# The queue that issues six stores in the opening of a gather, state-space and convolution kernel

## The chip, the core and the metric

The kernel runs on one NeuronCore of a Trainium2 chip. The core has five engines with an instruction queue each: TensorE (PE) multiplies matrices into PSUM, VectorE (DVE) and ScalarE (ACT) compute on PSUM and SBUF, GpSimd (POOL) computes on SBUF, and SyncE (SP) issues transfers. Each queue is worked off in order. Transfers between HBM and SBUF (DMAs) run on 16 DMA engines; in this kernel SP, ScalarE and GpSimd issue them.

The metric is the time of one execution in device microseconds. It was 1114.07 us in the median of three executions (1113.97 to 1115.91).

## The reference

The input `x` holds 64 batches of 128 channels by 2048 steps, all in float32. Two residual layers follow each other:

```
W = weights[condition]                         # one of 16 matrices [128, 128] for each batch
x = x + einsum('bct,bcd->bdt', x, W)           # layer 0
K = 2 Re( sum_n Ct[h,n] exp(dtA[h,n] * l) )    # layer 1: a kernel of 2048 taps for each channel
y = causal convolution of x with K, + x * D
x = x + y * (step < length[batch])
```

Layer 0 multiplies each batch by a matrix that an index selects. Layer 1 is a state-space layer: its convolution kernel is a sum of 64 damped exponentials for each channel.

## The kernel before

The 2048 steps are cut into two segments of 1024. Layer 0 is done batch by batch, and its result is written to a scratch tensor in HBM (`scr`) in a layout that the second layer reads by channel. Layer 1 works on eight-channel groups that it loads back from `scr`, with the states carried from chunk to chunk. TensorE does its transposes, its products with the Toeplitz matrix of near taps and its reads of the states.

The change touches the opening stage, in which segment 0 of layer 0 runs for all 64 batches and the tables of layer 1 are made beside it. The function `batch0(b)` is one batch of it:

- For an even `b` it calls `fetch` (line 443): SP issues the load of a pair of batches, 1 MB, that is used 18 batches later. Load number n holds batches 2n and 2n+1. There are ten such buffers (`big`, ten of tag `x`), so load n reuses the buffer of load n-10 and must wait until the stores of both its batches have landed.
- `weigh` (line 457): GpSimd copies the selected matrix of a later batch.
- `project` (lines 468 and 473 to 478): TensorE multiplies into a PSUM tile of two banks (tag `y`, two buffers), the function `copy` brings the result back into the batch's place in SBUF (line 475), and a DMA stores it to `scr` (line 478, 0.5 MB).

The copy is ScalarE's, except for batches 12 to 17, where it is VectorE's. In these six turns of the loop ScalarE computes tables of exponentials, two tables of four instructions each turn (`exps`, line 499, 48 instructions in all), and VectorE computes partial angles (`partial_angles`, lines 648 to 661). From batch 18 on a pipeline of small steps (`STEPS`) makes the sine tables, two batches to a table: TensorE transposes (line 666), ScalarE copies to `a` (line 670), TensorE multiplies (line 677), VectorE reduces the angles (lines 685 to 688), ScalarE takes the sines (lines 692 and 693), and so on.

The order of the work on each engine is that of the program. Semaphores between engines are placed by the compiler. For the DMAs that SP and ScalarE issue it has eight completion semaphores, which it gives out in turn in the order of issue; an issue waits until the DMA that had its semaphore before has landed.

The loop around the change, which calls `batch0` for batches 12 to 63, chooses the copying engine by the batch's number:

```
for now in range(12, B):
    batch0(now, V.tensor_copy if now < 18 else nc.scalar.copy)
    ...
    if now < 18:
        exps(2 * now - 20)
        exps(2 * now - 19)
```

Of the kernel before, what the change touches and what calls it, by code (L numbers as in the profile page):

```python
# [46 lines left out]
F32 = mybir.dt.float32  # L47
# [6 lines left out]
P = 128  # L54
# [322 lines left out]
def cond_resid_ssm_kernel(  # L377
# [13 lines left out]
    nc = tc.nc  # L391
# [9 lines left out]
    BK = 512  # L401
# [18 lines left out]
    psp = ctx.enter_context(tc.tile_pool(name="psp", bufs=1, space=PSUM))  # L420
# [14 lines left out]
    QB = SL // BK  # L435
# [3 lines left out]
    def fetch(s, n):  # L439

        xbs[s, n] = big.tile([P, BT, SL], F32, tag="x", name=f"xb_{s}_{n}")
        src = x[n * BT : (n + 1) * BT, :, s * SL : (s + 1) * SL]
        nc.sync.dma_start(xbs[s, n], src.rearrange("b c t -> c b t"))

    def weigh(s, b, plus=None):

        w1s[s, b] = s0.tile([P, C], F32, tag="w1", name=f"w1_{s}_{b}")
        at = nc.values_load(
            ci[:, b : b + 1],
            engines=(mybir.EngineType.Pool,),  # L450
            min_val=0,
            max_val=S - 1,
            skip_runtime_bounds_check_because="it is clamped above",
        )
        w = wres[:, bass.ds(at, 1), :].rearrange("p s d -> p (s d)")
        if plus is None:
            nc.gpsimd.tensor_copy(w1s[s, b], w)  # L457
        else:
            nc.gpsimd.tensor_tensor(w1s[s, b], w, plus, ALU.add)

    def project(s, b, q, ps, n_banks=1, copy=nc.scalar.copy):

        n, r = divmod(b, BT)
        own = xbs[s, n][:, r, :]
        for k in range(n_banks):
            cols = [slice((q + j) * BK, (q + j + 1) * BK) for j in (k, n_banks - 1 - k)]
            if s > 0:
                nc.tensor.matmul(ps[:, k], w1s[s, b], own[:, cols[0]], start=True, stop=True)  # L468
                continue

            for h in range(2):
                c = slice(h * B, (h + 1) * B)
                nc.tensor.matmul(ps[c, k], w1s[s, b][:, c], own[:, cols[h]], start=True, stop=True)  # L473
        cols = slice(q * BK, (q + n_banks) * BK)
        copy(own[:, cols], ps.rearrange("p k t -> p (k t)"))  # L475
        if q + n_banks == QB:
            to = scr[s].rearrange("(f b) c t -> b c f t", f=2)[b]
            nc.scalar.dma_start(to, own.rearrange("c (f t) -> c f t", f=2))
            del w1s[s, b]
            if r == BT - 1:  # L480
                del xbs[s, n]

    def batch0(b, copy=nc.scalar.copy):
        if b % BT == 0 and b // BT + AHEAD < B // BT:
            fetch(0, b // BT + AHEAD)
        if b + WAHEAD < B:
            weigh(0, b + WAHEAD)
        project(0, b, 0, psp.tile([P, QB, BK], F32, tag="y", name=f"p0_0_{b}", bufs=2), QB, copy)

    V = nc.vector  # L490
    es = [tab.tile([P, TP, 2, NE], F32, tag=f"e{g}", name=f"e_{g}") for g in range(NT)]
# [4 lines left out]
    def exps(g):  # L496

        for i in range(TP):
            nc.scalar.activation(es[g][:, i, 0, :], steps, AF.Exp, scale=par_of(DRE, g, i))
# [12 lines left out]
    with tc.tile_pool(name="setup", bufs=1) as setup:  # L512
# [93 lines left out]
        for b in range(3):  # L606
            batch0(b)
        par.sines()
        run(others)
        batch0(3)  # L610
        par.lay("ppar_1", rows, 3, par.row(gtab, DRE))
        run(par.gains())
        phases = _weave(par.phases(), masks(), par.steps_of_chunk())
        for b in range(4, 10):
            batch0(b)
            run(phases, 12)
            if b >= 6:
                exps(b - 6)
# [20 lines left out]
    def partial_angles(k):  # L639

        own = parts[:, :, 0:NL]
        by_l = some_l.unsqueeze(1).to_broadcast([P, NP, NL])

        def of(row, n):
            return gtab[:, row, :].unsqueeze(2).to_broadcast([P, NP, n])

        if k == 0:
            V.tensor_tensor(own, of(FHI, NL), by_l, ALU.mult)
        elif k == 1:
            V.tensor_scalar(whole, own, MAGIC, MAGIC, ALU.add, ALU.subtract)  # L650
        elif k == 2:
            V.tensor_tensor(own, own, whole, ALU.subtract)
        elif k == 3:
            V.tensor_tensor(whole, of(FLO, NL), by_l, ALU.mult)
        elif k == 4:
            V.tensor_tensor(own, own, whole, ALU.add)
        else:
            V.tensor_tensor(parts[:, :, 0:8], parts[:, :, 0:8], of(PHI, 8), ALU.add)
            V.tensor_tensor(parts[:, :, 24:25], parts[:, :, 24:25], of(PHI, 1), ALU.add)
            V.tensor_scalar(last, parts[:, :, 24:25], MAGIC, MAGIC, ALU.add, ALU.subtract)  # L660
            V.tensor_tensor(last, parts[:, :, 24:25], last, ALU.subtract)
# [76 lines left out]
    def some(n):  # L738
        nonlocal done
        for s, b, q in pieces[done : done + n]:  # L740
            weights_for(done + WAHEAD * QB + 1)
            project(s, b, q, psp.tile([P, 1, BK], F32, tag="tr", name=f"p0_{s}_{b}_{q}", bufs=2))
            done += 1

    def fetches(n):

        nonlocal begun
        while begun < min(n + BT * QB, len(pieces)):
            fetch(pieces[begun][0], pieces[begun][1] // BT)
            begun += BT * QB  # L750
# [9 lines left out]
    ps = {}  # L760
# [11 lines left out]
        0: turn_parts,  # L772
    }
    for now in range(12, B):
        batch0(now, V.tensor_copy if now < 18 else nc.scalar.copy)
        if now < 20:

            by_row = d_in.rearrange("(d c h j) -> c d j h", j=8, c=2, d=2)
            with nc.allow_non_contiguous_dma(reason="128 gains, four times"):
                for i, r in ((i, r) for i in range(TP) for r in range(4) if (i * 4 + r) // 2 == now - 12):  # L780
                    nc.gpsimd.dma_start(dcol[i * NR + r : (i + 1) * NR : 4, :], by_row[r % 2, r // 2])
        if now == 21:
            V.tensor_scalar(dcol, dcol, 1.0, None, ALU.add)
        if now < FIRST:
            partial_angles(now - 12)
# [3 lines that stand above are left out]
        for lag, step in STEPS.items():  # L789
            g, odd = divmod(now - FIRST - lag, 2)  # L790
            if not odd and 0 <= g < NT:
                step(g)
        if now == 60:
            fetches(FILL)
# [248 lines left out]
```

## Time and profile before

| | |
|---|---|
| median of three executions | 1114.07 us (1113.97 to 1115.91) |
| profiled execution: its own time | 1113.85 us |
| profiled execution: span | 1111.8 us |
| mean granted TensorE clock | 0.993 |
| busy: TensorE | 1070.2 us, 96% of the span |
| busy: VectorE | 817.7 us, 74% |
| busy: ScalarE | 679.9 us, 61% |
| busy: GpSimd | 226.9 us, 20% |
| DMA, mean over the span | 282 GB/s, 313.31 MB |
| stores to `scr` (line 478) | 128 of 0.5 MB, 7.8 us from issue to landing in the median |
| loads of pairs (line 443) | 64 of 1 MB, 9.6 us in the median |
| chain that ended last, by engine | TensorE 89%, DMA 6%, ScalarE 2%, VectorE 2% |

How to read it: times are counted from the start of the span. "Busy" leaves out instructions that only issue, branch or wait. The chain is followed back from the last instruction to what released it, or to the instruction before it on its engine. In the lists of instructions, columns are the start, the duration, engine, line, operation, what it writes and reads, the count, and in brackets the idle time before it with what ended it. "ACTq" and "SPq" are the queues of ScalarE and SP, in which DMAs are issued; "DMA scr<-xb" is a store, "DMA xb<-in_x_dram" a load.

### The profile page before, as it was taken

What the parts mean: (1) busy time and instruction counts of PE and PEld (TensorE: products, weight loads), DVE (VectorE), ACT (ScalarE), POOL (GpSimd) and SP (SyncE); (2) the same over time, 40 slices, a digit from 0 to 9 for tenths busy, and PEclk for the clock granted to TensorE, in tenths of its full rate; (3) what the DMA queues carried; (4) which work ended last, traced back from release to release, by engine and by line L of the source; (5) the groups of instructions that cost most, each with busy time, mean ns of one, the idle gap of its engine ahead of it and who ended that gap; (6) DMA issues with size and microseconds to landing.
All of it is one profiled execution on the core that took longest, in us unless ns stands there. A gap on an engine that the chain in (4) does not pass through costs nothing.

```text
span 1111.8 us, 24599 instructions
## 1 busy us (share of the span) xinstructions
PE 1070.2 (96%) x8890; PEld 756.9 (68%) x8890; DVE 817.7 (74%) x2902; ACT 679.9 (61%) x1119; POOL 226.9 (20%) x389
## 2 busy tenths in 40 slices
PE   4779999999999999999999999999999999999996
PEld 1223333667767777776776778788888888888885
DVE  7665650568667667766766868888888888888886
ACT  3576665666666666566666666555665566566552
POOL 3152342121121112122122111212111211111120
PEclk9799999999999999999999999999999999999999
DMA  9999999999999999999999877678777787888754
GB/s 345 414 398 397 386 383 369 402 332 284 353 297 292 298 314 287 306 311 289 294 306 299 255 236 230 213 210 246 223 219 219 241 229 212 229 235 228 208 166 119
DMA packets 142731, 313.31 MB, mean 282 GB/s; under 512 B 12882, under 2 KB 13010, under 8 KB 142610
## 3 DMA queue, kind: packets, MB, share of 16 engines
q1 hardware_dynamic: 96528, 218.65, 62.5%
q10 hardware_dynamic: 35106, 67.64, 15.9%
q0 software_dynamic: 10976, 25.45, 8.4%
q8 instruction: 70, 1.15, 0.4%
q14 instruction: 51, 0.42, 0.1%
HBM read 164.76 MB, written 146.93 MB: 280 GB/s over the span
## 4 chain that ended last, share of the span: by engine, by line
PE 89%; DMA 6%; ACT 2%; DVE 2%; issue 0%; ACTq 0%; SPq 0%; DVEq 0%
PE y L924 20%; PE y L916 20%; PE v L871 18%; PE tr L849 10%; PE p L468 9%; PE p L473 7%; DMA scr<-xb 3%; PE pb L832 2%; DMA xb<-in_x_dram 2%; PE pt L677 1%; DVE s L886 1%; ACT xb L475 1%; PE pk L707 1%; DMA x<-scr 1%; DVE x L946 1%; ACT s L876 0%
## 5 line engine op out<-in xcount | busy, mean ns | idle before, releaser
L886 DVE SCALAR_TENSOR_TENSOR s<-s,ptab 128x128 f32<-128x128 f32 x1792 | 536.5, 345 | 194.7 <-ACT s L876 194.5
L876 ACT ACTIVATE s<-v,ptab 64x512 f32<-64x512 f32 (+1 forms) x512 | 336.0, 656 | 52.0 <-PE v L871 34.9
L916 PEld LDWEIGHTS y<-tt,u 128*128 128x128 f32 x2048 | 263.5, 192 | 80.5 <-issue 67.0
L916 PE MATMUL y<-tt,u 128*128 128x128 f32 x2048 | 269.9, 275 | 0.1
L924 PEld LDWEIGHTS y<-e,s 64*128 64x128 f32 (+1 forms) x4096 | 219.0, 181 | 52.1 <-issue 27.2
L871 PE MATMUL v<-u,bt 128*128 128x512 f32 (+1 forms) x512 | 248.7, 567 | 1.3 <-ACT u L850 1.0
L850 ACT COPY u<-tr 128x512 f32<-128x512 f32 x252 | 148.1, 588 | 152.1 <-PE tr L849 125.6
L924 PE MATMUL y<-e,s 64*128 64x128 f32 (+1 forms) x4096 | 237.3, 276 | 1.4 <-DVE s L886 1.4
L475 ACT COPY xb<-p 128x512 f32<-128x512 f32 (+1 forms) x186 | 133.5, 718 | 85.9 <-PE p L468 54.4
L946 DVE COPY_PREDICATED x<-mask,y 128x1024 f32<-128x1024 uint8 x128 | 166.7, 1303 | 1.0 <-PE y L924 1.0
L849 PE MATMUL tr<-ident,x 128*128 128x128 f32 x1024 | 155.5, 274 | 1.2 <-DVE u L850 0.8
L849 PEld LDWEIGHTS tr<-ident,x 128*128 128x128 f32 x1024 | 121.2, 141 | 50.9 <-issue 44.9
L473 PE MATMUL p<-xb,w 128*64 128x512 f32 x512 | 126.0, 629 | 19.4 <-DMA xb<-in_x_dram 11.1
L457 POOL COPY w<-wres 128x128 f32 x125 | 56.7, 454 | 429.4 <-PE p L468 315.4
L468 PE MATMUL p<-xb,w 128*128 128x512 f32 x256 | 129.6, 596 | 0.9 <-issue 0.6
L473 PEld LDWEIGHTS p<-xb,w 128*64 128x64 f32 x512 | 35.4, 143 | 88.6 <-issue 84.9
L871 PEld LDWEIGHTS v<-u,bt 128*128 128x128 f32 x512 | 79.5, 191 | 15.9 <-issue 13.4
L818 POOL DMA_DIRECT2D tt<-kpad x64 | 50.5, 789 | 194.3 <-DVE s L886 158.3
L896 DVE TENSOR_SCALAR s<-s 128x64 f32<-128x64 f32 x448 | 87.8, 196 | 0.0
L859 POOL DMA_DIRECT2D s<-carry x64 | 44.9, 706 | 127.0 <-PE y L924 114.4
L833 ACT COPY bt<-pb 128x512 f32<-128x512 f32 x32 | 18.8, 586 | 79.3 <-PE pb L832 75.6
L907 POOL DMA_DIRECT2D carry<-s x64 | 43.6, 724 | 100.1 <-DVE s L886 88.3
(205 smaller groups left out, 390.1 us busy)
## 6 DMA issues: line engine op xcount, KB each, us to landing
xb<-in_x_dram SPq DMA_DIRECT2D x64, 1024.0 KB, 9.6
scr<-xb ACTq DMA_DIRECT2D x128, 512.0 KB, 7.8
x<-scr SPq DMA_DIRECT2D x64, 1024.0 KB, 8.2
out_dram<-x SPq DMA_DIRECT2D x130, 256.0 KB, 3.6
out_dram<-x SPq DMA_DIRECT2D x62, 512.0 KB, 4.6
tt<-kpad POOLq DMA_DIRECT2D x64, 256.0 KB, 5.7
btd<-bt SPq DMA_DIRECT2D x32, 256.0 KB, 5.2
bt<-btd SPq DMA_DIRECT2D x32, 256.0 KB, 4.8
```

Of the source, the lines that this page charges most:

```text
L468: nc.tensor.matmul(ps[:, k], w1s[s, b], own[:, cols[0]], start=True, stop=True)
L473: nc.tensor.matmul(ps[c, k], w1s[s, b][:, c], own[:, cols[h]], start=True, stop=True)
L475: copy(own[:, cols], ps.rearrange("p k t -> p (k t)"))
L849: nc.tensor.transpose(tr[:, k, :], xs[i][:, n, k * Q : (k + 1) * Q], ident)
L850: (nc.vector.tensor_copy if i == 0 else nc.scalar.copy)(u, tr)
L871: nc.tensor.matmul(v[:, 0:nv], w, us[i, n].rearrange("p k r -> p (k r)")[:, 0:nv], start=True, stop=True)
L876: nc.scalar.activation(own[:, 0:nv], v[lanes, 0:nv], AF.Copy, scale=amp)
L886: nc.vector.scalar_tensor_tensor(new, src, factor, own, ALU.mult, ALU.add)
L896: nc.vector.tensor_scalar(old[d][:, 2], old[d][:, 0], -1.0, None, ALU.mult)
L916: nc.tensor.matmul(y[:, k, :], u[:, k, :], tts[i][:, n, :], start=(k == 0), stop=False, skip_group_check=True)
L924: nc.tensor.matmul(ys[i, d][rows, c, k, :], ss[i][half[c], d, part, k, :, :].rearrange("p f b -> p (f b)")[:, rows], es[pair // TP][half[c ...
L946: nc.vector.copy_predicated(xs[i][:, 2 * d : 2 * d + 2, :].rearrange("r c (k t) -> r c k t", k=KK), keep_k.unsqueeze(1).to_broadcast([P, 2 ...
```

## The change

The six stores of batches 12 to 17 are issued by SP. The function `project` gets a parameter for the queue that issues the store, `batch0` hands it on, and the loop passes `nc.sync` for the batches that VectorE copies. The copies, the loads, the sizes and the order of everything else in the program stay as they are.

```diff
-    def project(s, b, q, ps, n_banks=1, copy=nc.scalar.copy):
+    def project(s, b, q, ps, n_banks=1, copy=nc.scalar.copy, queue=nc.scalar):
 ...
         if q + n_banks == QB:
             to = scr[s].rearrange("(f b) c t -> b c f t", f=2)[b]
-            nc.scalar.dma_start(to, own.rearrange("c (f t) -> c f t", f=2))
+            queue.dma_start(to, own.rearrange("c (f t) -> c f t", f=2))
 ...
-    def batch0(b, copy=nc.scalar.copy):
+    def batch0(b, copy=nc.scalar.copy, queue=nc.scalar):
 ...
-        project(0, b, 0, psp.tile([P, QB, BK], F32, tag="y", name=f"p0_0_{b}", bufs=2), QB, copy)
+        project(0, b, 0, psp.tile([P, QB, BK], F32, tag="y", name=f"p0_0_{b}", bufs=2), QB, copy, queue)
 ...
     for now in range(12, B):
-        batch0(now, V.tensor_copy if now < 18 else nc.scalar.copy)
+        if now < 18:
+            batch0(now, V.tensor_copy, nc.sync)
+        else:
+            batch0(now)
```

## The prediction

> In what follows "store 14" is the store of batch 14 (line 478) and "fetch 17" the load of batches 34 and 35 (line 443). All durations come from the profiled execution: span 1111.8 us, time 1113.85 us, which is 0.22 below the median of 1114.07.
>
> **What bounds the kernel now.** I read the chain of waits first, in order of time, around the six batches:
>
> ```profile
> 50.77 11.13 DMA scr<-xb
> ...
> 61.98 0.03 SPq L443
> ...
> 62.04 7.67 DMA xb<-in_x_dram
> ...
> 69.79 0.37 ACTq L478
> ...
> 72.66 0.91 ACT xb L475
> ```
>
> Columns are start, duration, what. Store 11 takes 11.13 us to land; SP then issues fetch 15 at 62.04, which waited for it because it reuses the buffer of batches 10 and 11. Fetch 15 lands at 69.72, and only then does ScalarE issue store 17 (69.79). So a store waits for a fetch's landing. The records of the DMA issues name their completion counters: eight are used in turn by both hardware queues, and an issue waits until the DMA eight places before it has landed. From fetch 15 the order of issue is stores 12 and 13, fetch 16, stores 14 and 15, fetch 17, stores 16 and 17; store 17 is the eighth.
>
> Next, ScalarE's timeline:
>
> ```profile
> 50.77 4.19 ACTq L478 DMA_DIRECT2D scr<-xb  x2
> 54.99 1.28 ACT L499 ACT_TABLE_LOAD   x1 [7.79 <-DVE xb L475]
> ...
> 70.21 2.46 ACT L499 ACTIVATE e<-steps,gtab 128x129 f32<-128x129 f32 x8 [1.73 <-DMA xb<-in_x_dram]
> 72.57 0.99 ACT L475 COPY xb<-p 128x1024 f32<-128x1024 f32 x1
> ```
>
> Store 12 sits ahead of the exponentials and waits for VectorE's copy; store 17 holds the last eight. The copy of batch 18 starts at 72.57, though its matmuls were over long before, as TensorE's timeline shows:
>
> ```profile
> 65.30 1.94 PE L473 MATMUL p<-xb,w 128*64 128x512 f32 x8 [0.88 <-issue]
> 68.90 0.33 PE L666 MATMUL pa<-ident,parts 128*128 128x128 f32 x1 [1.66 <-DVE parts L659]
> 69.16 1.94 PE L473 MATMUL p<-xb,w 128*64 128x512 f32 x8
> 73.66 1.94 PE L473 MATMUL p<-xb,w 128*64 128x512 f32 x8 [2.56 <-issue]
> ...
> 86.56 1.12 PE L677 MATMUL pt<-pick,a 128*128 128x512 f32 x2 [0.77 <-ACT a L670]
> ```
>
> These are batches 18, 19 and 20, and the last row is TensorE's last idle moment. The busy times by stretch say what comes after:
>
> ```profile
> 86.00:160.00 74.00, 73.44 (x463) 23.99 (x465) 43.39 (x92) 49.79 (x81) 23.65 (x49) 1.00 1.03 386
> ```
>
> TensorE (first figure after the length) is busy 73.44 of 74 us. Whatever the start of this stretch gains or loses goes to the end unchanged. In the stretch before it the 16 DMA engines are busy throughout as well:
>
> ```profile
> DMA packets 7462, 17.70 MB, mean 402 GB/s; under 512 B 929, under 2 KB 929, under 8 KB 7458
> ```
>
> **The change part by part.**
>
> *ScalarE loses six issues and their waits.* Store 11 stays there (50.77 to 51.23). The table load (1.28) and 48 exponentials follow at once. From 56.29 to 72.57 they took 16.28 us, of which 1.73 and 0.24 were waits: (16.28 - 1.97)/48 = 0.30 each, 14.3 together. They end near 51.2 + 1.3 + 14.3 = 66.9 in place of 72.57. Batch 18's matmuls end at 67.2, so its copy runs from 67.2 to 68.2. Batch 19's matmuls don't move (69.16, behind VectorE's row L659). Batch 20's need the PSUM buffer of batch 18 and would start at 71.1 instead of 73.66. Taken alone: -2.6 us.
>
> *SP gains six issues* of 0.37 us, 2.2 us; SP otherwise waits (44.1 us for store landings between 48 and 92), so the issues as such cost nothing. Without that cover they would cost those 2.2 us.
>
> *The stores stand in line behind fetches that wait.* In SP's program store 12 comes after fetch 15 (`batch0` fetches first), store 14 after fetch 16, store 16 after fetch 17, fetch 18 after store 17. Fetch 15 can't go before 62.0, as store 11 still lands at 61.9. Stores 12 and 13 therefore go at 62.4 and 62.9 and not at 54.60 and 57.46. Fetch 16 reuses the buffers of batches 12 and 13 and waits for both to land; stores 14 and 15 stand behind it, and so on. A pipeline becomes three round trips.
>
> *The price of one round trip* is a fetch and two stores through one queue with nothing beside them. Data: 2.1 MB at the 402 GB/s above is 5.2 us (2.6 + 1.3 + 1.3). The part that doesn't scale: the shortest landing of a store before 200 us is 3.2, less 1.3, so 1.9. Together 7.1, against a pace of 5.5 before (86.56 to 92.03, two batches). Where ScalarE's own stores are in flight, one of them adds 1.3.
>
> - stores 12, 13 landed: 62.0 + 7.1 = 69.1; fetch 16 issued 69.2 (before: 65.87)
> - fetch 17: 69.2 + 7.1 + 1.3 (store 18 beside it) = 77.6 (before: 71.05)
> - fetch 18: 77.6 + 7.1 + 1.3 = 86.0 (before: 76.30); it lands 1.9 + 2.6 + 0.6 later, at 91.1
>
> *Who waits for them.* Fetch 18 feeds batch 36, some five pairs later (about 117), so TensorE doesn't miss the data. ScalarE does: by the rule of eight, store 19 waits for fetch 16 to land (69.2 + 5.1 = 74.3; before it went at 75.04, so -0.7), store 21 for fetch 17 (82.7; 80.24, +2.5), store 23 for fetch 18 (91.1; 85.83, +5.3). Behind store 23 on ScalarE is the copy `a` of line 670, which the matmul at 86.56 waits for. The gain of 2.6 is thus eaten at store 19, and the path that sets the end is +5.3.
>
> The order of issue of before is one end. With the exponentials early, store 18 may take a place ahead of fetch 18, and every counter behind shifts by one: store 24 and not 23 waits for fetch 18. Before, it went at 87.45. Without store 18 beside the second round, fetch 18 lands nearer 90; store 24 is then 2.5 late, and the matmul two batches on had about 1.3 to spare between them: +1.2. With other shifts the waits fall on stores 20 to 26, between these two. I can't tell the order from this trace and take the middle: (1.2 + 5.3)/2 = **+3.2**.
>
> *A rule that speaks to this.* The Trainium skill, page "DMA: Bandwidth & Descriptors", section "Rules for kernel authors", says that spreading DMAs over SP, ACT and GpSimd brings no bandwidth and saves only the sequencer's time of issue. By it the change would be worth at most ScalarE's six issues, 2.2 us by the 0.37 row, and 1111.6 would come out. The rows 61.98 and 69.79 show what the rule leaves out: what the issue waits for in its line.
>
> *After the stretch* nothing is added: fetches 19 and 20 follow fetch 18 at once (86.4, then when store 21 has landed, near 88; before 80.72 and 88.60).
>
> Sum: 1113.85 + 3.2 = 1117.05, with 0.22 to the median **1117.3 us**; the case's own range is 1115.3 (+1.2) to 1119.4 (+5.3).
>
> **Rivals.**
>
> *Faster: ScalarE is free and nothing holds its stores.* For it: the exponentials' head start of 5.7 us, and TensorE's 2.56 idle before batch 20. Against it: the counter wait is in the trace at 69.79. It needs fetch 18 to land by 83, and that means rounds of some 5.3 us, the pace of a queue that never drains. Time: 1113.85 - 2.6 + 0.2 = 1111.5. 10%.
>
> *No change: gain and waits meet.* If the order shifts and a round costs 6.5, fetch 18 lands two microseconds sooner and store 24 goes on time: 1113.5 to 1115. 13%.
>
> *Much slower: the rounds run at loaded latency.* Fetches between 86 and 160 take 7.3 to 9.4 us to land with ScalarE's stores beside them. With 9.4 a round, fetch 18 goes at 62.0 + 3 x 9.4 = 90.2, lands near 96, and store 23 is 10 late: 1124, or 1121 if the order shifts. Against it: in the first round ScalarE's queue is empty, and in the other two it holds one or two stores. 7%.
>
> **How the numbers follow.** The forecast has 70%. What a measurement of this kernel can tell from no change is 0.2%, 2.2 us: below 1111.8, above 1116.3. Of the forecast's range from +1.2 to +5.3 about three quarters lie beyond +2.2: 0.53, and with the much slower case 0.60. Faster: 0.08 (the rival's -2.6 lies just beyond the bound). Same: 0.32. Range for 8 in 10: it cuts off most of the faster case and half of the much slower one, 1113.4 to 1120.6.
>
> **What would show it.** Right: stores 12 and 13 issued by SP after 62, both landed near 69; fetches 16, 17, 18 near 69, 77 and 86; the copy of batch 18 near 67; an idle ScalarE of several us before a store between 21 and 24; TensorE's steady stretch beginning 1 to 5 us later than 86.56, and the same shift at the end. Wrong: fetch 18 issued before 80, or no ScalarE wait at a counter after 75; or a shift in the steady stretch that is gone by 190, when the first transposes start.

## The result and the profile after

The changed kernel takes 1124.1 us in the median of five executions (1120.97 to 1125.58), the kernel before beside it 1115.91 (1113.97 to 1117.92). The ratio is 1.0072, with a 95% interval from 1.0055 to 1.009: some 8 us slower. The prediction had the direction, the round trips and the kind of wait that costs, and less than half of the size: 1117.3, with a range up to 1120.6.

The profiled execution of the changed kernel took 1124.1 us with a span of 1122.3; granted clock 0.987, TensorE busy 1075.1 us (1070.2 before). Line numbers behind 778 are three higher than before.

First the chain of waits (start, duration, what):

```profile
51.34 11.10 DMA scr<-xb
62.57 0.37 SPq L443
63.03 0.42 SPq L478
63.51 8.44 DMA scr<-xb
72.03 0.37 SPq L443
72.46 0.46 SPq L478
73.02 9.46 DMA scr<-xb
82.55 6.71 DMA xb<-in_x_dram
89.34 0.37 ACTq L478
...
93.93 1.13 PE pt L677 x2
```

These are the serial round trips: fetch 15, stores 12 and 13, their landing, fetch 16, stores 14 and 15, their landing, fetch 17 and its landing, and only then a store of ScalarE. From fetch to fetch it takes 9.46 us (62.57 to 72.03) and 10.52 (72.03 to 82.55).

Fetch 18 does not wait for the third round, as SP's timeline shows (its last row merges six loads, the first of them fetch 18):

```profile
82.55 0.37 SPq L443 DMA_DIRECT2D xb<-in_x_dram  x1
82.98 1.15 SPq L478 DMA_DIRECT2D scr<-xb  x2
84.23 28.26 SPq L443 DMA_DIRECT2D xb<-in_x_dram  x6
```

Stores 16 and 17 land at 91.19 and 92.44, but fetch 18 goes at 84.23. By the semaphores that the issues name, it has the buffer of batches 18 and 19 here, whose stores have landed by 80.96, and fetch 19, at 92.50, has that of batches 16 and 17. Load n reuses the buffer of load n-10 in the kernel before, but not for these two loads of the changed kernel. Why the buffers are given out in another order, no run shows.

ScalarE's timeline shows the gain and what ate it (idle time before an instruction and its releaser in brackets):

```profile
53.46 14.18 ACT L499 ACTIVATE e<-steps,gtab 128x129 f32<-128x129 f32 x48
67.55 0.98 ACT L475 COPY xb<-p 128x1024 f32<-128x1024 f32 x1
...
79.05 1.01 ACT L475 COPY xb<-p 128x1024 f32<-128x1024 f32 x1 [4.68 <-DMA xb<-in_x_dram]
...
83.05 0.27 ACT L670 COPY a<-pa 128x128 f32<-128x128 f32 x1 [2.98 <-DMA scr<-xb]
...
89.73 1.28 ACT L692 ACT_TABLE_LOAD   x1 [5.50 <-DMA xb<-in_x_dram]
```

All 48 exponentials run in one piece and batch 18's copy starts at 67.55, five microseconds earlier than before. Then three of ScalarE's own stores wait at the shared completion counters: store 20 for fetch 16's landing, store 21 for store 15's (82.48), store 22 for fetch 17's (89.26). ScalarE is idle for 4.68, 2.98 and 5.50 us before what stands behind each of them. No store of ScalarE waits for fetch 18: from 93.20 on each goes as soon as its copy is done. TensorE waits for `a`:

```profile
83.37 2.07 PE L677 MATMUL pt<-pick,a 128*128 128x512 f32 x2 [5.04 <-ACT a L670]
...
85.58 5.54 PE L473 MATMUL p<-xb,w 128*64 128x512 f32 x16
...
93.93 1.13 PE L677 MATMUL pt<-pick,a 128*128 128x512 f32 x2 [2.80 <-ACT a L670]
```

The last row is the matmul that stood at 86.56 before: 7.37 us late. Between the waits the clock is at half for a while (the 16 matmuls of two batches in 5.54 us), but TensorE still has to wait 2.80 us behind them, so that costs nothing here. The busy times by stretch (length, TensorE, its weight loads, VectorE, ScalarE, GpSimd, clock, DMA share, GB/s):

```profile
50.00:75.00 25.00, 20.86 (x78) 6.15 (x78) 17.00 (x19) 18.55 (x53) 15.42 (x23) 0.89 0.87 301
75.00:86.00 11.00, 5.96 (x21) 1.88 (x19) 2.09 (x5) 2.19 (x3) 0.59 (x2) 0.85 0.89 293
100.00:160.00 60.00, 60.00 (x386) 19.57 (x385) 35.87 (x77) 40.46 (x67) 20.38 (x42) 1.00 1.03 397
```

The first two stretches before:

```profile
50.00:75.00 25.00, 18.86 (x72) 5.48 (x69) 16.46 (x17) 17.59 (x51) 15.25 (x22) 0.90 1.03 404
75.00:86.00 11.00, 10.23 (x42) 2.99 (x38) 5.22 (x10) 6.91 (x10) 1.24 (x5) 1.00 1.03 394
```

They moved 404 and 394 GB/s. The changed kernel moves 103 x 25 + 101 x 11 = 3.7 MB less in them, 9.1 us of the DMA engines at 404. From 100 on TensorE is busy 60.00 of 60 us, so nothing is caught up. A second loss comes where the second layer starts (line 852 transposes the first tile that is read back from `scr`, `x_0`; the first two rows are of the kernel before, where it is line 849):

```profile
189.23 6.85 DMA x<-scr
196.22 0.63 PE L849 MATMUL tr<-ident,x 128*128 128x128 f32 x4 [0.45 <-DMA x<-scr]
...
197.13 8.34 DMA x<-scr
205.61 1.08 PE L852 MATMUL tr<-ident,x 128*128 128x128 f32 x4 [2.51 <-DMA x<-scr]
207.48 1.11 PE L852 MATMUL tr<-ident,x 128*128 128x128 f32 x4 [0.79 <-DVE u L853]
208.39 1.91 PE L874 MATMUL v<-u,bt 128*128 128x512 f32 x2
...
212.49 0.60 PE L852 MATMUL tr<-ident,x 128*128 128x128 f32 x4
```

TensorE waits 2.51 us for `x_0` (0.45 before). The load of `x_0` is issued 7.90 us later than before, of which 7.33 are TensorE's own lateness, and takes 1.49 longer to land. Then four transposes take 1.1 us where four take 0.60 some microseconds later: the clock is halved for a while. By the times of before, the offset to its profile grows from 7.33 at 193 to 9.39 at the first transposes and 12.09 at 205; near 720 it falls by 1.5, where VectorE held TensorE up before and no longer does. It ends at 10.57.

### The profile page after: what moved, and what is told of

Same layout as the page of the kernel before. It is cut to its first block, busy times and chain, and to the rows that moved or that the text cites. A ratio compares the mean times of both kernels' runs of the same rounds, so it can differ in the third digit from the quotient of the medians.

```text
span 1122.3 us, 24596 instructions
## 1 busy us (share of the span) xinstructions
PE 1075.1 (96%) x8890; PEld 759.1 (68%) x8890; DVE 817.5 (73%) x2902; ACT 678.9 (60%) x1119; POOL 225.1 (20%) x389
## 4 chain that ended last, share of the span: by engine, by line
PE 89%; DMA 7%; DVE 1%; ACT 1%; issue 0%; SPq 0%; ACTq 0%; DVEq 0%
PE y L927 20%; PE y L919 20%; PE v L874 18%; PE tr L852 11%; PE p L468 9%; PE p L473 7%; DMA scr<-xb 5%; PE pb L835 2%; DMA xb<-in_x_dram 1%; PE pt L677 1%; PE pk L707 1%; DMA x<-scr 1%; DVE s L889 1%; ACT xb L475 0%; DVE x L949 0%
```

## The experiments

Ratios are to the kernel before on the same chip, with 95% intervals. Line numbers move by a few with each edit. "Offset" is the start of an instruction of TensorE less that of the same instruction in the first profile of before.

**1. The order on SP alone.** The stores stay with SP, but no store stands behind a fetch that waits for stores.

```diff
-    def batch0(b, copy=nc.scalar.copy, queue=nc.scalar):
-        if b % BT == 0 and b // BT + AHEAD < B // BT:
+    def batch0(b, copy=nc.scalar.copy, queue=nc.scalar, load=True):
+        if load and b % BT == 0 and b // BT + AHEAD < B // BT:
 ...
-            batch0(now, V.tensor_copy, nc.sync)
+            batch0(now, V.tensor_copy, nc.sync, load=False)
+            for n in {15: (15,), 17: (16, 17)}.get(now, ()):
+                fetch(0, n)
```

> Stores 12 to 17 stay on SP, but fetch 15 is issued after store 15 and fetches 16 and 17 after store 17, so that no store stands behind a fetch that waits for a landing. Line theory (the loss comes from stores standing behind waiting fetches): stores 12 and 13 go near 55 and 58 as in the kernel before, fetch 17 before 73 and fetch 18 before 80, no wait of ScalarE over 2 us before stores 20 to 23, steady stretch from 84 to 88, time 1111 to 1116. Sharing theory (loads and stores in one hardware queue are what is slow, in whatever order): rounds of 9 us and more remain, steady stretch from 92 or later, 1120 to 1125.

Measured: 1112.2 us, ratio 0.9953 (0.9933 to 0.9973). The steady stretch begins 3.43 us earlier than before, fetch 18 goes at 73.41. Its busy times in the two stretches:

```profile
50.00:75.00 25.00, 20.08 (x82) 6.04 (x80) 16.19 (x16) 18.55 (x53) 16.49 (x23) 0.96 1.04 404
75.00:86.00 11.00, 10.13 (x42) 3.00 (x38) 6.93 (x15) 8.15 (x11) 1.17 (x4) 1.00 1.04 412
```

The same stores in the same queue move 404 and 412 GB/s and the loss is gone. The place of the stores in SP's line is the cause; that loads and stores share a queue is not. The kernel is faster than both others. Of the 3.43 us it keeps 0.66 in its profile: TensorE waits 1.77 us for `x_0` and runs at half clock after it.

**2. The six stores on GpSimd.**

```diff
-            batch0(now, V.tensor_copy, nc.sync)
+            batch0(now, V.tensor_copy, nc.gpsimd)
```

> The six stores are issued by GpSimd. Line theory and sharing theory both: nothing stands behind a waiting fetch on SP and ScalarE is free, so the exponentials end near 67, fetch 18 goes before 80, steady stretch from 84 to 87, time 1110 to 1115. If it is ScalarE's early exponentials that do the harm (copies of batches 18 to 20 come earlier and crowd the transfers): steady stretch later than 90, 1119 or more.

Measured: 1119.49 us, ratio 1.0033 (1.0018 to 1.0049). The first expectation missed. The time is that of the second, but early exponentials are not the reason: experiment 1 has them as well and is faster. TensorE was 5.02 us early at 76, as foreseen, and 2.83 late from 92 on. VectorE's timeline says why:

```profile
82.66 0.17 DVE L786 TENSOR_SCALAR dcol<-dcol 128x4 f32<-128x4 f32 x1 [15.44 <-DMA dcol<-in_L_cond_D_dram]
```

GpSimd also issues small gathers (`dcol`, 0.1 KB each). Issued behind the 0.5 MB stores in its queue they took up to 12 us to land (5.0 in the median before), and VectorE's next step waits for the last of them. The stores found another line to hold up.

**3. Only the first round blocked.** Stores 12 and 13 on SP, 14 to 17 on ScalarE.

```diff
-            batch0(now, V.tensor_copy, nc.sync)
+            batch0(now, V.tensor_copy, nc.sync if now < 14 else nc.scalar)
```

> Only stores 12 and 13 are issued by SP, behind fetch 15; stores 14 to 17 by ScalarE. Line theory: one round trip of 9 to 10 us in place of three, fetch 16 near 72, and ScalarE's exponentials late again behind store 14 to 17; steady stretch 1 to 5 us later than before, time 1115 to 1119. Sharing theory: a third of the loss, 1116 to 1119 as well; if one blocked round were to cost as much as three: 1121 or more.

Measured: 1119.24 us, ratio 1.0027 (1.0013 to 1.0041); offset of the steady stretch 5.12, at the edge of the expectation. Fetch 16 goes at 74.17, a round of 12.11 us with stores of ScalarE beside it, but fetches 17 and 18 follow at 74.65 and 75.59, before fetch 18's old time of 76.30. Still ScalarE is held, by the landings of store 13 (1.86 us at 74.67) and of fetches 16 and 17:

```profile
84.46 0.37 ACTq L478 DMA_DIRECT2D scr<-xb  x1
84.87 0.27 ACT L670 COPY a<-pa 128x128 f32<-128x128 f32 x1 [2.87 <-DMA xb<-in_x_dram]
```

So a late fetch 18 is not needed for a loss; one late round is enough.

**4. Only the last round blocked.** Stores 16 and 17 on SP, 12 to 15 on ScalarE.

```diff
-            batch0(now, V.tensor_copy, nc.sync)
+            batch0(now, V.tensor_copy, nc.sync if now > 15 else nc.scalar)
```

> Only stores 16 and 17 are issued by SP, behind fetch 17; 12 to 15 by ScalarE. Fetches 15, 16 and 17 go as before (62, 66, 71), only fetch 18 waits for a round trip. If fetch 18 alone were what holds ScalarE, as the prediction reckoned: fetch 18 near 81, a wait of ScalarE before a store behind it, steady stretch 2 to 6 us late, time 1117 to 1122. If the loss comes from fetches 16 and 17 and the lost transfer time of the first rounds: steady stretch within 1.5 us of before, time 1113 to 1118.

Measured: 1118.27 us, ratio 1.0011 (0.999 to 1.0032), which does not tell it from no change. The profile of one execution shows more: fetches 15 to 17 go at 62.02, 65.88 and 70.94, fetch 18 at 82.39, and ScalarE's timeline has

```profile
90.71 0.37 ACTq L478 DMA_DIRECT2D scr<-xb  x1
91.13 0.63 ACT L692 ACTIVATE t<-t 128x516 f32<-128x516 f32 x1 [5.39 <-DMA xb<-in_x_dram]
```

It waits for fetch 18's landing (90.64). TensorE goes from 1.68 us early to 3.70 late, so the second reading of the expectation, that the loss lies in fetches 16 and 17 and the first rounds alone, falls. This is the prediction's own case, a late fetch 18 for which a store of ScalarE waits, at about the predicted +3.2. Experiment 4 has one such hold of ScalarE, experiment 3 and the changed kernel have three.

**5. ScalarE away from the shared counters.** The changed kernel, with stores 18 to 25 on GpSimd, whose DMAs have counters of their own.

```diff
-            batch0(now)
+            batch0(now, queue=nc.gpsimd if now < 26 else nc.scalar)
```

> The changed kernel, with stores 18 to 25 issued by GpSimd so that ScalarE's copies wait at no shared counter; the three slow round trips on SP remain. Counter theory (TensorE is late because ScalarE waits at the counters before stores 20 to 22): fetches 16 and 17 still near 72 and 82, but the steady stretch begins at 84 to 88, time 1111 to 1118. Data theory (the fetches themselves come too late for TensorE): steady stretch from 91 or later, 1120 to 1125.

Measured: 1118.37 us, ratio 1.002 (1.0006 to 1.0033). The round trips are as slow as ever (fetch 16 at 71.60, fetch 17 at 84.27), but TensorE is 3.64 us early at 76 and only 0.61 late from 92 to 101. What it loses between them is the wait of experiment 2 again, as two of the stores stand ahead of gathers in GpSimd's queue:

```profile
81.15 0.17 DVE L786 TENSOR_SCALAR dcol<-dcol 128x4 f32<-128x4 f32 x1 [11.85 <-DMA dcol<-in_L_cond_D_dram]
```

Then comes the first of ScalarE's own stores that meets a late fetch:

```profile
106.74 0.37 ACTq L478 DMA_DIRECT2D scr<-xb  x1
107.15 0.27 ACT L670 COPY a<-pa 128x128 f32<-128x128 f32 x1 [4.87 <-DMA xb<-in_x_dram]
```

From there the offset is 7.07. As the median and the profiled execution (1121.03) were apart, the kernel ran once more:

> The changed kernel with stores 18 to 25 on GpSimd, once more, for a second profile: its median was 2 us above the kernel before, its profiled execution 7. If that execution was typical in what it shows (TensorE on time until 100, then a wait of ScalarE of 4 us or more at the first of its own stores that meets a late fetch): the same wait again, 1117 to 1122. If it was an outlier: no wait over 2 us of ScalarE between 95 and 115, steady stretch within 2 us of the kernel before to 180, 1115 to 1118.

Measured: 1120.38 us, ratio 1.0033 (1.0017 to 1.005), the same picture: 0.90 late until 104, then waits of 1.95 and 3.94 us at ScalarE's stores, 3.96 late. The counters are what makes TensorE late at 83 and 94 in the changed kernel. Taken away there, the wait moves to the next store that shares them, because the fetches stay late: the counter theory has the place and not the whole size. By the ratios, 0.20% and 0.33% are left of 0.72%.

**6. No store of ScalarE in the whole stage.** As 5, but for all batches from 18 on, to see whether late transfers alone delay `x_0`.

```diff
-            batch0(now, queue=nc.gpsimd if now < 26 else nc.scalar)
+            batch0(now, queue=nc.gpsimd)
```

> The changed kernel, with the stores of all batches from 18 to 63 issued by GpSimd, so that no counter shared with a fetch can hold ScalarE anywhere in the stretch; the three slow round trips on SP remain. Transfer theory (up to the first read of the scratch tensor the transfers are as tight as TensorE, so what they lose between 58 and 86 comes back there whatever TensorE does): steady stretch from 84 to 88 and on time until 180, but the first transposes of x_0 at 203 to 206, with 6 us of idle TensorE or more ahead of them, time 1119 to 1124. TensorE theory (x_0 is late only because TensorE is): first transposes at 192 to 198, time 1110 to 1115.

Measured: 1133.99 us, ratio 1.0162 (1.0123 to 1.0201), and nothing for the question: the offset is 0.23 until 109, then TensorE waits again and again for what depends on GpSimd's queue, and the offset is 19.39 at `x_0`. ScalarE alone waits 35.4 us between 100 and 195 for small stores that GpSimd issues (`kpad`). GpSimd's queue had become the bound.

**7. Transfers added to the kernel before.** Eight more copies of 0.5 MB on GpSimd's queue, from the input to a tensor that nobody reads.

```diff
+    extra = dram.tile([8, P, SL], F32, tag="extra", name="extra")
 ...
+        if 30 <= now < 46 and now % 2 == 0:
+            nc.gpsimd.dma_start(extra[(now - 30) // 2], x[now - 30, :, 0:SL])
```

> The kernel before with 8 more transfers of 512 KB, from the input to a scratch tensor that nobody reads, issued by GpSimd on its own queue between 100 and 140 us: 4.2 MB, some 10 us of the DMA engines at 410 GB/s, of which the stretch's free share (388 of 410 GB/s over 100 us, some 5 us) can take half. No store stands behind anything new. Transfer theory (up to x_0 the transfers are as tight as TensorE): TensorE within 1.5 us of its old times until 180, then first transposes of x_0 3 to 9 us later, time 1118 to 1126. TensorE theory (transfers have slack; x_0 is late only when TensorE is): first transposes within 1.5 us of before, time 1113 to 1117.

Measured: 1123.06 us, ratio 1.0071 (1.0052 to 1.0091). So 4.2 MB, 10.4 us of the DMA engines at 404 GB/s, cost some 8 us, the loss of the changed kernel for 3.7 MB. The place was not the one expected: TensorE is held inside the stretch (offset 1.49 from 76 to 109, 9.58 from 158 on), not at `x_0` alone.

```profile
100.00:140.00 40.00, 36.79 (x242) 12.05 (x242) 22.89 (x49) 23.79 (x41) 16.05 (x34) 1.00 1.03 400
140.00:186.00 46.00, 43.18 (x268) 13.99 (x264) 19.11 (x41) 27.32 (x43) 15.16 (x34) 0.96 1.03 399
```

TensorE is busy 79.97 of 86 us here, 85.69 before. ScalarE's stores take 9.5 to 14.9 us to land between 108 and 152 (4.5 to 8.3 before), and between 100 and 165 ScalarE waits five times, 12.7 us in all, for the landing of a fetch. So added transfers are paid in this stage, and they are paid at the same counters. That the changed kernel pays at `x_0` for the transfer time that it lost in the opening is not shown by this: of the 9.39 us by which `x_0` comes late there, 7.33 are TensorE's own lateness.

**8. The price of a round trip by itself.** Fetches 15 to 17 as two loads of 0.5 MB each; looked at for the first round alone.

```diff
-        nc.sync.dma_start(xbs[s, n], src.rearrange("b c t -> c b t"))
+        if s == 0 and 15 <= n <= 17:
+            for r in range(BT):
+                nc.sync.dma_start(xbs[s, n][:, r], src[r])
+        else:
+            nc.sync.dma_start(xbs[s, n], src.rearrange("b c t -> c b t"))
```

> The changed kernel with fetches 15, 16 and 17 issued as two loads of 512 KB each. Looked at for the first round alone, since the counters shift behind it: fetch 15 goes at 62 into empty queues. Start theory (empty queues need some microseconds before data flows at 400 GB/s, however many loads are given): both halves landed 6 to 7 us after the first issue, like the one load of 1 MB (6.52), stores 12 and 13 near 72. Single load theory (one load alone is served slower than several): both halves landed within 5 us, stores 12 and 13 near 70.5.

Measured (1121.46 us, one execution): by the records of the DMA issues the first halves of the three fetches landed 4.91, 4.95 and 4.98 us after their issue, the second half of fetch 15 at 67.98, 6.15 after the first's issue. Whole loads into drained queues took 6.52 (changed kernel), 6.54 and 6.44 (experiment 5) and 6.50 us (experiment 6; fetch 15 in each). The start theory has the loads right (6 to 7 us). The round ended earlier than it said, with fetch 16 at 70.64, where the other theory had it: 8.81 us after fetch 15, 9.46 in the changed kernel. As an estimate, half a megabyte more costs 6.52 - 4.95 = 1.57 us, so the part that does not grow with the size is 4.95 - 1.57 = 3.4 us; the first half had the second beside it, so a half alone may land sooner.

**9. The halved clock.** The changed kernel with 16 more transposes into the tile of `x_0`'s first ones; their results are overwritten.

```diff
+        for k in range(16 if (i, n) == (0, 0) else 0):
+            nc.tensor.transpose(tr[:, k % KK, :], es[0][:, 0, 0, 1:NE], ident)
```

> The changed kernel with 16 more transposes of 128 x 128, some 2.4 us, into the PSUM tile of x_0's first transposes, while TensorE waits for x_0; their results are overwritten. Clock theory (the halved clock after the idle 2.5 us costs the 2.7 us between 205 and 216): granted clock 1.0 from the first transposes on, offset to before 9.4 in place of 12.1, time 2 to 3 us under the changed kernel's 1124.1. If the 2.7 us are something else (VectorE's copies, late weights): no change, 1123 to 1125.

Measured: 1121.48 us, ratio 1.005 (1.0036 to 1.0064), 2.6 us under the changed kernel's median; the intervals of the two ratios overlap a little. TensorE's timeline:

```profile
202.26 1.97 PE L852 MATMUL tr<-ident,e 128*128 128x128 f32 x16 [0.20 <-ACT xb L475]
204.07 1.04 PE L854 MATMUL tr<-ident,x 128*128 128x128 f32 x8
```

Eight transposes take 1.04 us where four took 1.08. The granted clock from 196 to 212 is 1.00 (0.80 in the changed kernel), and the offset does not grow behind the first transposes (7.85, then 7.42). In that execution the halved clock is gone and with it the 2.7 us.

The same with 12 transposes in the kernel of experiment 1:

> The kernel with fetch 15 behind store 15 and fetches 16 and 17 behind store 17, with 12 more transposes ahead of x_0's first ones as a filler. Clock theory: the halved clock at 195 is gone, 1.4 us less than that kernel's 1112.2, ratio to the kernel before 0.993 to 0.996. Otherwise: the same ratio as without the filler, 0.995, or worse if the filler runs past the landing of x_0.

Measured: 1112.02 us, ratio 0.9964 (0.9949 to 0.9978), against 0.9953 without: no difference in the median. The profile has the clock at 1.00 and an offset of -1.65 in place of -0.66, less than what executions differ by. Experiment 1 is the version to keep.

**10. The kernel before, again.**

> The kernel before, unchanged, for a second profile: the first one, 1113.85, lies at the fast end of its executions (median 1116.4). Either the difference lies in the stretch up to 94 (steady stretch begins 2 to 3 us later than 86.56, so that the changed kernel's 7.4 is 5 in the median), or at x_0's first transposes and the halved clock behind them (steady stretch as before, 2 to 3 us more between 195 and 212), or it is spread over the rest.

Measured: 1114.89 us, ratio 0.9988 (0.9966 to 1.0009), profiled execution 1115.33. The steady stretch begins 0.28 us from the first profile's, but

```profile
198.59 0.63 PE L849 MATMUL tr<-ident,x 128*128 128x128 f32 x4 [2.02 <-DMA x<-scr]
```

TensorE waits 2.02 us for `x_0` here, 0.45 in the first profile; the offset is 2.39 behind it and 1.47 at the end. So the kernel before has this wait too in some executions, and the first profile flattered it. Against this one, the changed kernel's 9.1 us (span 1122.3 less 1113.2) are 7.1 up to 180, -0.6 near 185, 0.5 up to the first transposes, 2.7 from there to 205, the size of the halved clock, and -0.6 near 720.

## Why the prediction was wrong, point by point

- **ScalarE's gain**: right. Exponentials to 67.6 (predicted 66.9), copy of batch 18 at 67.55 (67.2). TensorE was 2.54 us early at 76 (2.8 to 5.0 in experiments 1, 2 and 5); the prediction had 2.6.
- **Stores 12 and 13 behind fetch 15**: right, at 63.03 and 63.51 (62.4 and 62.9). Experiment 1 shows that this order is the cause.
- **The price of one round trip**: the term that failed. The prediction put 7.1 us, 8.4 with a store of ScalarE beside. Measured, from fetch to fetch, 9.46 and 10.52, and 9.95 to fetch 19 at 92.50, the one that had waited for stores 16 and 17. The three sum to 29.9 where 23.9 were reckoned. The part that doesn't scale was taken from the shortest landing of a store, 1.9; for a load into drained queues it is 3.4 (experiment 8). With 3.4 the first round is 8.6. The rest is small steps: fetch 15 alone took 6.52 and not 3.4 + 2.6 = 6.0, and the stores behind it landed 1.55 and 1.30 later. So fetch 17 landed at 89.26, where the sum had 82.7.
- **Who waits**: right in kind. The trace could not tell which stores; it was 20, 21 and 22, inside the 20 to 26 of the text. But the forecast's delay came from fetch 18, and in the changed kernel no store of ScalarE waited for its landing. That fetch 18 went at 84.23, near the 86.0 of the sum, was luck: it had another buffer and went right behind the issue of store 17, with no third round to wait for. With dearer rounds fetches 16 and 17 hold ScalarE in its place, and experiment 3 shows that they do even with fetch 18 on time. Experiment 4, with fetch 18 alone late, has the mechanism at the forecast's size, +3.70. TensorE's delay was 7.37 in place of 3.2, with 5.3 as the upper end.
- **After the stretch nothing is added**: wrong. TensorE caught nothing up, as foreseen, but at `x_0` the idle time brought the halved clock, 2.7 us (9.39 to 12.09), which the profile of before, with 0.45 us of idle time there, did not show. The text had read the transfers as busy throughout, yet not drawn from it what more of them would cost; transfers added behind the opening are paid (experiment 7).
- **The rivals**: "much slower: the rounds run at loaded latency" was given 7% and 1121 to 1124, and came out at 1124.1. Its price of 9.4 a round was about right. The objection to it, that ScalarE's queue is empty in the first round, did not make that round cheap: it took 9.46 with empty queues, and the next two 10.52 and 9.95 with stores of ScalarE beside them.
- **The Trainium skill's rule** (page "DMA: Bandwidth & Descriptors", section "Rules for kernel authors") that spreading DMAs over queues saves only issue time would have made 1111.6 of this change (1111.9 with the 0.22 to the median). Experiment 1, with the stores on SP, moves 404 and 412 GB/s in the two stretches, 404 and 394 before, which agrees with it; what an issue stands behind is outside the rule, and cost some 8 us.

What stays open: why a load into drained queues needs 3.4 us beyond its data, where a store needs 1.9; and whether the transfer time lost in the opening costs anything by itself. Experiments 5 and 7 show late or added transfers only where they hold ScalarE at the counters.

## What to carry to other kernels

Before a DMA is moved to another queue, write down what stands ahead of it there and what that waits for: a store behind a load that waits for the store before it turns a pipeline into round trips, and putting the loads behind the stores in the same queue undid it and gained 0.47% (0.9933 to 0.9973) over the kernel before. Price such a round from a transfer of the same kind in drained queues, not from the bandwidth of a full one. Where engines share completion counters, a late load holds up an engine that has no use for its data.

## What the hardware showed that was not expected

Data starts slowly in drained queues. Busy times of the changed kernel by single microseconds (last two figures: DMA share, GB/s):

```profile
62.00:63.00 1.00, 0.38 (x2) 0.23 (x4) 1.00 (x2) 1.00 (x5) 1.00 (x2) 1.00 0.06 17
63.00:64.00 1.00, 1.00 (x8) 0.34 (x4) 1.00 (x1) 1.00 (x4) 1.00 (x1) 1.00 0.58 45
64.00:65.00 1.00, 0.55 (x4) 0.00 (x0) 1.00 (x2) 1.00 (x5) 1.00 (x3) 1.00 0.76 172
65.00:66.00 1.00, 0.56 (x4) 0.34 (x6) 1.00 (x2) 1.00 (x5) 1.00 (x2) 1.00 0.91 274
...
69.00:70.00 1.00, 0.88 (x5) 0.47 (x7) 0.55 (x3) 0.00 (x0) 0.98 (x2) 1.00 1.06 404
```

Fetch 15 is issued at 62.57. Three microseconds later the engines count as nearly busy, but move 274 GB/s; 400 comes only at 69, when the stores are under way. A busy share near 1 is therefore no proof of full bandwidth.

The Trainium skill's page "DMA: Bandwidth & Descriptors" has two figures for this: the fit in its section "Anatomy of one DMA" gives 2.0 us and the bytes at 436 GB/s, 4.4 us for 1 MB as an estimate, while the table in "Bandwidth" has 6.15 us for 1 MB. Both are for transfers that GpSimd issues, and the table counts only the time in which the DMA engines are busy. The loads of this case, issued by SP, took 6.44 to 6.54 us from issue to landing and lie nearer the table.

The clock was halved after idle times of 2.51 us in front of `x_0` (changed kernel), 2.49 (experiment 2), 2.02 (experiment 3), 1.95 (second run of experiment 5) and 1.77 (experiment 1), and stayed full after 2.02 (experiment 10) and 1.70 (first run of experiment 5): the length alone does not decide. The Trainium skill's page "TensorE: Matmul & The Clock Gate", section "Part 1: The HAM clock gate", tells of a free-running window of about 3.4 us that must be idle, and its table of advice warns of gaps over some 3 us. A free-running window agrees with the scatter; the limit does not, as 1.77 us sufficed here, with 0.63 us of work and 0.78 of idle time behind it.
